# Four output tiles moved from cross-attention into the last self-attention unit, and context keys padded with zeros, in a transformer block on one core

## The chip, the core and the metric

The kernel runs on one core of a Trainium2 chip, in float32 throughout. A time is that of one execution on the device, in microseconds (us); smaller is better. A profile is one execution recorded by the hardware. Its engines are PE (TensorE, matmuls), PEld (its weight loads, beside the matmuls), DVE (VectorE), ACT (ScalarE), POOL (GpSimd) and SP (SyncE, which issues most DMAs).

## What is computed

One transformer block with 16 heads of 64, on x of 2 x 1024 x 256 and a context of 2 x 154 x 192. The inner width of attention is 1024, the feed-forward's is 1024 with a gate.

```python
def _attention(xq, xkv, wq, wk, wv, wo, bo):
    q = (xq @ wq).reshape(B, S, N_HEADS, D_HEAD)
    k = (xkv @ wk).reshape(B, T, N_HEADS, D_HEAD)
    v = (xkv @ wv).reshape(B, T, N_HEADS, D_HEAD)
    attn = softmax(einsum('bihd,bjhd->bhij', q, k) * D_HEAD ** -0.5)
    out = einsum('bhij,bjhd->bihd', attn, v).reshape(B, S, D_ATTN)
    return out @ wo + bo

h = _layernorm(x, ln1_g, ln1_b)
x = _attention(h, h, sa_wq, sa_wk, sa_wv, sa_wo, sa_bo) + x
h = _layernorm(x, ln2_g, ln2_b)
x = _attention(h, cond_emb, ca_wq, ca_wk, ca_wv, ca_wo, ca_bo) + x
h = _layernorm(x, ln3_g, ln3_b)
a, gate = split(h @ ff_w1 + ff_b1)
x = (a * gelu(gate)) @ ff_w2 + ff_b2 + x
```

## The kernel before

All of x stays on chip, as tiles of 128 rows (8 for each of the two batch entries, `xt`), and the three stages run one after the other. Work is cut into units: one batch entry and one pair of heads, 16 units for each attention.

**Self-attention** is a loop over `p` of 128 slots, 8 for each unit, and a slot takes 2 groups of 64 query rows. In `self_first` PE makes the scores (L370) into both buffers of the PSUM pool `ps_s`, DVE takes their maxima over half of the keys (L530), and ACT the exponents with their sums (L381), which frees the scores' banks for the next slot. Two halves of the keys lie on different partitions, so each slot sends maxima and sums to its neighbours by four small DMAs on SP (`exchange`, L391), and a slot later `join` reconciles them: differences on POOL (L399 to L401), the exponent `ee` on ACT (L403), sums on POOL (L405, L407), the reciprocal `rd` on DVE (L477), and POOL weighs the exponents (L481). A slot after that DVE transposes them in 32x32 blocks (L495), and PE multiplies them with the values (`self_values`, L417) in the slots p with p % 4 of 2 or 3. In the slots with p % 4 of 0 or 1 `run_work` gives PE other work: pieces of the next unit from the list `work` (two halves of the queries `q`, the keys, the values), one step of the normalisation that the next stage needs (`side`), and output tiles of attention (`outs`, `out_piece`: four matmuls of 128x256, L348, and a DVE add into x, L355). Banks for these come from the PSUM pool `ps_m`, two buffers. What a piece leaves for ACT is run in the next slot (`stores`), what it leaves for DVE too (`adds`). One closure of `later` is run in each slot; the bias adds on POOL (L255) are among them.

**Cross-attention** is a loop over `c` of 48 slots, 3 for each unit, and a slot takes up to 3 tiles of 128 query rows. Here the scores (L645) are one matmul for each tile and head, 154 wide, followed by maxima (`neg`, L650), exponents (L661), reciprocal (L669), weighing (L672) and transposes into 32x32 blocks (L688). The first five slots also finish the last slots of self-attention (`self_drain`): the weighing of slot 127 in c = 0, its transposes in c = 1, its values in c = 2 and 3. The 154 keys are padded to 5 blocks of 32 in the exponents. For each two pairs of heads the values of the context are made in one piece (`values`, L604 to L619): a memset on POOL of the last block's tile, matmuls for 128 and for 26 rows, and three ACT copies, the last into the memset's tile; then DMAs bring the rows to the other partitions (L621, L626).

The order on every engine is that in which the program emits the instructions: there is no scheduler behind it[...]. The last unit of self-attention is p = 120 to 127. At p = 120 `self_beside` takes the pieces of the first unit of cross-attention:

```python
            work.extend(nxt[:2])
            held.extend(nxt[2:])
```

`held` joins `work` at p = 124. A slot of that unit runs one piece:

```python
                full = hg % 2 == 0 or outs and p < SA - 2 * SH
                run_work(2 if full and p < SA - 2 * SH else 1, 1, sum_tile)
```

So it has q0 in slot 120, q1 in 121, the keys in 124 and the values in 125. Tiles 4 to 7 of the first half of batch entry 1's output come to `outs` at c = 0 (`out_pieces("sa", B - 1, 0, range(NT // 2, NT))`), and the slots of cross-attention take two pieces each, `work` first: one tile in slot 1, two in slot 2, one in slot 4. The heads that they sum were done before the last unit.

The stages that follow are the feed-forward, 64 slots (L809, L815, L818, L832), with the outputs of cross-attention among them.

The names: S = 1024, P = 128, T = 154, KB = 32, NB = 5, NT = 8, SH = 4, SA = 128, NPAIR = 8, CC = 96, VC = 256, NM = 2.

## Time and profile before

| | |
|---|---|
| median of 3 runs | 1179.57 us (1178.59 to 1180.47) |
| the profiled execution | 1178.48 us |
| its span | 1176.6 us |
| PE busy | 1143.3 us (97%) |
| DVE, POOL, ACT busy | 830.9 (71%), 670.7 (57%), 642.9 (55%) us |
| matmuls of the scores (L370) and values (L417) | 256.4 and 236.3 us |
| matmuls of output tiles (py_sa, L348) | 256 records, median 379 ns |
| exponents (L381), weighing (L481) | 345.2 us of ACT, 387.6 us of POOL |
| maxima (L530), transposes (L495) | 301.4 and 302.4 us of DVE |
| granted clock of PE over the span | 0.994 |

The span runs from the first to the last instruction; what lies around it belongs to the execution's own time. A row of the timeline gives the start, the time from its first to its last instruction, the engine, the line, the operation, what is written and read with its size, and the count; brackets hold the idle time of the engine before it and what ended it. A float32 matmul is two records here, so that a tile's four matmuls show as x8. In a row of stretches a busy time is followed by the number of instructions, and 1.00 is the full clock of PE.

### The profile page before, as it was taken

To read this page: it belongs to the slowest core of one execution; us is meant where nothing else is said; L and a number is where in the kernel's file an instruction comes from. 1 tells how busy PE (TensorE), PEld (TensorE's weight loads), DVE (VectorE), ACT (ScalarE), POOL (GpSimd) and SP (SyncE) were. 2 spreads that over 40 slices of the span, in tenths; PEclk is the share of its full clock that TensorE was granted. 3 is DMA by queue.
4 is the path that set the end of the run, shared out by engine and by line. 5 is a ranking of instruction groups with operands and counts; after the bars stand their busy time and mean duration, and the time that the engine had idled before them with its cause. 6 is when DMAs were issued, how large, how long until landed. Compare 5 with 4: busy or idle time off the path is not lost.

```text
span 1176.6 us, 31689 instructions
## 1 busy us (share of the span) xinstructions
PE 1143.3 (97%) x11907; PEld 669.7 (57%) x11907; DVE 830.9 (71%) x1172; ACT 642.9 (55%) x2053; POOL 670.7 (57%) x1563
## 2 busy tenths in 40 slices
PE   7999999999999999999999988999999999999998
PEld 4434445545545545545545433665555567888887
DVE  3888888898888888889999888556655574232222
ACT  3656776666656656656666765456655572041111
POOL 1678777877777777777777777445644453030000
PEclk8999999999999999999999998999999999999999
DMA  2321011011111111111111110176444433000000
GB/s 63 92 61 27 18 27 21 22 33 21 26 25 22 24 25 21 28 22 21 28 23 21 24 21 6 46 173 156 102 107 102 102 80 73 1 19 9 18 10 18
DMA packets 87018, 51.06 MB, mean 43 GB/s; under 512 B 30742, under 2 KB 77650, under 8 KB 86866
## 3 DMA queue, kind: packets, MB, share of 16 engines
q1 hardware_dynamic: 83650, 46.42, 17.4%
q10 hardware_dynamic: 3216, 2.62, 0.7%
q8 instruction: 94, 1.54, 0.6%
q14 instruction: 58, 0.48, 0.1%
HBM read 19.52 MB, written 2.10 MB: 18 GB/s over the span
## 4 chain that ended last, share of the span: by engine, by line
PE 75%; POOL 6%; ACT 6%; DMA 4%; DVE 4%; issue 3%; SPq 2%; ACTq 0%; DVEq 0%; POOLq 0%
PE po L417 14%; PE s L370 13%; PE pa L809 9%; PE py_sa L348 5%; PE py_ca L348 5%; PE pf L832 5%; PE pq_ca L290 4%; ACT p L381 4%; PE poc L721 4%; DMA st<-st 3%; PE pk_sa L290 3%; PE pq_sa L290 3%; PE sc L645 3%; PE pv_sa L305 3%; POOL p L481 3%
## 5 line engine op out<-in xcount | busy, mean ns | idle before, releaser
L381 ACT ACTIVATE p<-s,st 128x512 f32<-128x512 f32 x512 | 345.2, 686 | 219.9 <-DVE st L530 210.4
L481 POOL TENSOR_SCALAR p<-p,rd,ee 128x512 f32<-128x512 f32 x512 | 387.6, 772 | 43.8 <-DVE rd L477 43.2
L530 DVE TENSOR_REDUCE st<-s 128x2 f32<-128x1024 f32 x256 | 301.4, 1219 | 45.9 <-PE s L370 38.1
L495 DVE STREAM_TRANSPOSE pT<-p 128x1024 f32<-128x1024 f32 x256 | 302.4, 1218 | 0.6 <-POOL p L481 0.5
L370 PE MATMUL s<-k_sa,q_sa 64*32 64x512 f32 x4096 | 256.4, 600 | 20.5 <-ACT p L381 19.3
L417 PE MATMUL po<-pT,v_sa 64*64 64x256 f32 x4096 | 236.3, 380 | 1.2 <-DVE pT L495 1.2
L417 PEld LDWEIGHTS po<-pT,v_sa 64*64 64x64 f32 x4096 | 151.0, 133 | 110.5 <-issue 40.4
L672 POOL TENSOR_SCALAR p<-p,rden 128x154 f32<-128x154 f32 x256 | 97.4, 402 | 119.3 <-DVE rden L669 118.1
L370 PEld LDWEIGHTS s<-k_sa,q_sa 64*32 64x32 f32 x4096 | 58.8, 106 | 153.8 <-ACT p L381 67.8
L661 ACT ACTIVATE p<-sc,neg 128x154 f32<-128x154 f32 x256 | 96.0, 394 | 88.6 <-DVE rden L669 84.4
L809 PE MATMUL pa<-hT_ln,wf 128*128 128x256 f32 x512 | 121.0, 379 | 0.0
L818 DVE SCALAR_TENSOR_TENSOR u<-pa,cols,gate 128x256 f32<-128x256 f32 x64 | 31.0, 484 | 124.1 <-ACT gate L815 124.1
L815 ACT ACTIVATE gate<-pa,cols 128x256 f32<-128x256 f32 x64 | 30.3, 474 | 152.1 <-PE pa L809 152.1
L809 PEld LDWEIGHTS pa<-hT_ln,wf 128*128 128x128 f32 x512 | 96.8, 190 | 13.7 <-issue 0.8
L381 ACT ACTIVATION_READ_ACCUMULATOR p<-s,st 128x1 f32 x512 | 103.5, 202 | 0.0
L650 DVE TENSOR_REDUCE neg<-sc 128x6 f32<-128x924 f32 (+1 forms) x48 | 48.6, 1013 | 48.3 <-PE sc L645 48.3
L405 POOL TENSOR_TENSOR zz<-ee,st 128x8 f32<-128x8 f32 x128 | 26.0, 203 | 84.3 <-ACT ee L403 84.3
L305 PEld LDWEIGHTS pv_sa<-sa_wv,hT_ln 128*128 128x128 f32 x512 | 59.3, 192 | 16.3 <-issue 12.9
L832 PE MATMUL pf<-wf,u 128*128 128x256 f32 x256 | 65.0, 379 | 0.2 <-DVE u L818 0.2
L305 PE MATMUL pv_sa<-sa_wv,hT_ln 128*128 128x128 f32 x512 | 62.4, 278 | 0.0
L290 PE MATMUL pq_sa<-hT_ln,sa_wq 128*128 128x512 f32 x128 | 61.2, 621 | 0.6 <-DVE hT_ln L230 0.6
L290 PE MATMUL pk_sa<-hT_ln,sa_wk 128*128 128x512 f32 x128 | 60.7, 610 | 1.2 <-DVE hT_ln L230 1.2
(73 smaller groups left out, 1228.4 us busy)
## 6 DMA issues: line engine op xcount, KB each, us to landing
wf<-pT_ca SPq DMA_DIRECT2D x128, 128.0 KB
st<-st SPq DMA_DIRECT2D x512, 1.0 KB
v_sa<-v_sa SPq DMA_DIRECT2D x64, 128.0 KB
wf<-in_L_xattn_ff_w_dram SPq DMA_DIRECT2D x12, 256.0 KB
sa_wq<-in_L_xattn_sa_wq_dram SPq DMA_DIRECT2D x16, 128.0 KB
sa_wk<-in_L_xattn_sa_wk_dram SPq DMA_DIRECT2D x16, 128.0 KB
sa_wv<-in_L_xattn_sa_wv_dram SPq DMA_DIRECT2D x16, 128.0 KB
ca_wq<-in_L_xattn_ca_wq_dram SPq DMA_DIRECT2D x16, 128.0 KB
```

The costliest lines, as they stand in the source:

```text
L290: nc.tensor.matmul(pq, lhsT=wt[:, c, :], rhs=h[:, c, n * HB:(n + 1) * HB], start=(c == 0), stop=(c == NC - 1),)
L305: nc.tensor.matmul(pv[:, i * P:(i + 1) * P], lhsT=h[:, c, (n * GT + i) * P:(n * GT + i + 1) * P], rhs=wt[:, c, :], start=(c == 0), stop=(c ...
L348: nc.tensor.matmul(py[:, :D], lhsT=o[:, i, t * P:(t + 1) * P], rhs=wo[kind][:, half * HP + i, :], start=(i == 0), stop=(i == HP - 1),)
L370: nc.tensor.matmul(sc[a4 * KB:(a4 + 1) * KB, j, :], lhsT=q[r, c:c + KB], rhs=k[r, h * HB:(h + 1) * HB], start=True, stop=True, tile_positi ...
L381: nc.scalar.activation(pr[:, j, :], sc[:, j, :], AF.Exp, bias=st[:, 0, 0, i, j:j + 1], accum_out=st[:, 0, 1, i, j:j + 1],)
L417: nc.tensor.matmul(po[a2][j * DH:(j + 1) * DH, :QH // 2], lhsT=v[r, t, e, j * DH:(j + 1) * DH], rhs=pT[r, j * NK + n, :], start=(t == 0 an ...
L481: nc.gpsimd.tensor_scalar(pr[:, j, :], pr[:, j, :], rd[:, c:c + 1], ee[:, 0, c:c + 1], op0=ALU.mult, op1=ALU.mult,)
L495: nc.vector.transpose(halves[h][:, :, c:c + KB], groups.pop(0).rearrange("p j (n k) -> p (j n) k", k=KB))
L530: nc.vector.tensor_reduce(st[:, 0, 0, i, :], sc[i], AX.X, ALU.max, negate=True)
L672: nc.gpsimd.tensor_scalar(pr_[:, j, i, :T], pr_[:, j, i, :T], rden[:, j, i:i + 1], 1.0, op0=ALU.mult, op1=ALU.mult,)
L809: nc.tensor.matmul(pa[:, half, :TF * P], lhsT=w1[:, c, half * DF + f * P:half * DF + (f + 1) * P], rhs=h[:, c, t0 * P:(t0 + TF) * P], star ...
L832: nc.tensor.matmul(sums[blk][i][:, :D], lhsT=sums[blk, "u"][:, f, i * P:(i + 1) * P], rhs=w2[:, f, :], start=(f == 0), stop=(f == NF - 1),)
```

## The change

- The padded length TP = 160 replaces T = 154 as the step between the batch entries in the transposed context `ctxT`, and all of `ctxT` is set to zero once at the start, on POOL. The values of the last block come out as zeros beyond row 154, so its matmul, copy and DMAs take 32 rows, and the memset in `values` goes.
- The maxima of cross-attention (`neg`) use the buffers of the tag "zz", 4 wide, in place of their own.
- The four output tiles go into `work` and `held` at p = 120, two and two. The slots of the last unit with p % 4 of 0 or 1 run two pieces each: q0 and q1; tiles 4 and 5; keys and values; tiles 6 and 7. Slot c = 0 runs one piece in place of two.

```diff
+    TP = NB * KB
...
-    ctxT = const.tile([CC, 2, B * T], F32, tag="ctxT", name="ctxT")
+    ctxT = const.tile([CC, 2, B * TP], F32, tag="ctxT", name="ctxT")
+    nc.gpsimd.memset(ctxT, 0.0)
...
-            ctxT[:, :, b * T:(b + 1) * T], pc[:CC, :2 * T].rearrange("p (c k) -> p c k", c=2)
+            ctxT[:, :, b * TP:b * TP + T], pc[:CC, :2 * T].rearrange("p (c k) -> p c k", c=2)
...
-            work.extend(nxt[:2])
-            held.extend(nxt[2:])
+            spare["out"] = mm_tile
+            last = [lambda t=t: out_piece("sa", B - 1, 0, t) for t in range(NT // 2, NT)]
+            work.extend(nxt[:2] + last[:2])
+            held.extend(nxt[2:] + last[2:])
...
-                    rhs=ctxT[:, c, b * T:(b + 1) * T], start=(c == 0), stop=(c == 1),
+                    rhs=ctxT[:, c, b * TP:b * TP + T], start=(c == 0), stop=(c == 1),
...
-            nc.gpsimd.memset(v[:, NM, :], 0.0)
             pv = mm_tile(f"pv_ca{b}_{pr}")
-            m = T - P
-            for n, rows_ in ((0, P), (1, m)):
+            for n, rows_ in ((0, P), (1, KB)):
...
-                        lhsT=ctxT[:, c, b * T + n * P:b * T + n * P + rows_],
+                        lhsT=ctxT[:, c, b * TP + n * P:b * TP + n * P + rows_],
...
-                nc.scalar.copy(v[:m, NM, :], pv[:m, VC:])
+                nc.scalar.copy(v[:KB, NM, :], pv[:KB, VC:])
...
-                    nc.sync.dma_start(out=v[a4 * KB:a4 * KB + m, NM, :], in_=v[:m, NM, :])
+                    nc.sync.dma_start(out=v[a4 * KB:(a4 + 1) * KB, NM, :], in_=v[:KB, NM, :])
...
-        neg = small.tile([P, 2, TG], F32, tag="neg", name=f"neg_{c}")
+        neg = small.tile([P, 2, 4], F32, tag="zz", name=f"neg_{c}")
...
-                full = hg % 2 == 0 or outs and p < SA - 2 * SH
-                run_work(2 if full and p < SA - 2 * SH else 1, 1, sum_tile)
+                full = hg % 2 == 0 or outs or p >= SA - 2 * SH
+                run_work(2 if full else 1, 1, sum_tile)
...
-            if c == 0:
-                out_pieces("sa", B - 1, 0, range(NT // 2, NT))
...
-            run_work(2, 1, n_sum=2 * (SH < c < 2 * NPAIR and c % len(CG) == 0))
+            run_work(2 if c else 1, 1, n_sum=2 * (SH < c < 2 * NPAIR and c % len(CG) == 0))
```

## The prediction

> **What bounds the kernel now.** I read the page first (PE busy 97% of the span, but dips in two slices of the transition from self- to cross-attention), then busy time by stretch over that transition, then the timelines of PE, ACT and POOL inside it, then the granted clock in 1.2 us steps. "Slot p" is one turn of the self-attention loop (p = 120 to 127 is the last unit), "slot c" one of the cross-attention loop. In the stretches the columns are us, then busy us of PE, PEld, DVE, ACT, POOL, the granted clock and DMA.

> ```profile
> 687.61:735.93 48.32, 40.35 (x537) 16.14 (x533) 39.52 (x41) 27.60 (x85) 38.09 (x86) 0.93 0.05 10
> 735.93:764.88 28.95, 27.77 (x244) 18.74 (x241) 14.98 (x24) 13.43 (x60) 14.51 (x37) 1.00 0.15 45
> 764.88:805.00 40.12, 40.12 (x281) 26.32 (x282) 23.78 (x57) 18.85 (x90) 17.40 (x54) 1.00 0.72 178
> ```

> The first row is the last unit: PE is idle for 8.0 of 48.3 us, and POOL and DVE lead. The second is c = 0 to 4: PE idle for only 1.2 us. The third has no idle at all. So PE work is free in the first stretch and sets the end in the other two, where DVE, ACT and POOL are half idle.

> ```profile
> 714.62 1.09 PE L370 MATMUL s<-k_sa,q_sa 64*32 64x512 f32 x16 [2.34 <-ACT p L381]
> ...
> 717.85 2.78 PE L609 MATMUL pv_ca<-ca_wv,ctxT 96*128 96x256 f32 x8
> ...
> 728.58 1.16 PE L370 MATMUL s<-k_sa,q_sa 64*32 64x512 f32 x16 [2.43 <-ACT p L381]
> ...
> 731.80 4.20 PE L417 MATMUL po<-pT,v_sa 64*64 64x256 f32 x64
> ...
> 745.95 3.68 PE L417 MATMUL po<-pT,v_sa 64*64 64x256 f32 x64 [1.18 <-DVE pT L495]
> ...
> 749.56 3.72 PE L348 MATMUL py_sa<-sa_wo,o_sa 128*128 128x256 f32 x16
> ...
> 763.06 1.89 PE L348 MATMUL py_sa<-sa_wo,o_sa 128*128 128x256 f32 x8
> 764.88 0.79 PE L645 MATMUL sc<-k_ca,q_ca 64*128 64x154 f32 x8
> ```

> PE waits for exponents ahead of the scores; two output tiles (x16) stand in slot 2 and one (x8) in slot 4, back to back with the rest.

> ```profile
> 721.85 0.73 ACT L618 COPY v_ca<-pv_ca 64x256 f32<-64x256 f32 x2
> 726.83 0.36 ACT L619 COPY v_ca<-pv_ca 26x256 f32<-26x256 f32 x1 [4.25 <-POOL v_ca L604]
> ```

> ```profile
> 725.81 0.73 POOL L255 TENSOR_TENSOR x<-x,ca_bo 128x256 f32<-128x256 f32 x1
> 726.48 0.32 POOL L604 MEMSET v_ca<- 128x256 f32 x1
> ```

> The memset costs 0.32 us but stands on POOL behind 3.03 us of weighing (L481) and a bias add. ACT's third copy waits 4.25 us for it, and the exponents of slot 126 are queued behind that copy. DVE's maxima start 5.50 us apart from slot 120 to 126 (689.85, 695.35, ... 722.85) and then 8.01 us apart (730.86): the stall costs 2.5 us.

> **The memset and the padding.** Eight memsets leave POOL, 8 x 0.32 = 2.6 us, where POOL has slack; only the first matters, for the 2.5 us above (the others are waited for by 0.5 us in all). The new one, 96x640, stands at the start between the memset of the identity and its select. The identity's memset (128x128) takes 0.20 and the 128x256 one 0.32, so 0.12 per 128 columns: 0.20 + 4 x 0.12 = 0.7 us, an estimate. The warming transposes would then end near 7.3 in place of 6.6, and PE's next work starts at 9.35, released by ACT: hidden by that 2.7 us gap, 0.7 us if it were gone. A shorter gap could also spare some of the half clock that this profile shows from 9.2 to 16.0; between -1.8 (the first query projection takes 3.75 us there, 1.98 later) and +0.7 I take 0, nearest to the gap's row. The values' second matmul, its copy and its three DMAs get 32 rows for 26[...], so no cost. The maxima's tile now rotates with another of four buffers; its earlier users are over two slots old: nothing.

> **The four tiles.** A tile is 1.82 to 1.86 us of PE (3.66 for two, from 749.56 to 753.22) and a DVE add of 0.38 to 0.43. Two go to slot 121 and two to 125, and q1 and the values move up a slot, so slots 120 and 124 hold two pieces. PE's idle time ahead of scores was 1.39, 1.39, 2.59 and 2.60 = 8.0 us in that unit; the tiles need 7.3. Filled, slot 121 runs scores to 695.0, tiles to 698.7, and the next scores, free of their banks at 698.1, come 0.5 us late; DVE needs them only at 700.86. A slot with two pieces is 1.9 + 3.65 = 5.55 us against the loop's 5.50: no loss. Without the idle time the move would only shift 7.3 us.

> The adds stand on DVE ahead of the reciprocal, which POOL's weighing waits for. In slot 122 DVE has 2.36 + 2.36 + 0.8 + 0.2 = 5.7 us of work: +0.2. In slot 126 the same, and that bounds it, for the bias add (0.73) has left POOL's slot 125. So the maxima of slot 126 start at 723.05, those of 127 at 723.05 + 5.7 = 728.75, where it was 730.86: 2.1 us won. PE's last values of the unit end at 731.95, against 735.93: PE is 4.0 us ahead.

> **What is late next.** Slot 2's values (745.95 before) need the transposes of slot 127, and that chain is not shortened by fewer tiles. From 728.75: exponents end 732.7; POOL weighs slot 126 from 733.85 to 736.85; the bias add, moved here, 0.7; differences to 738.45; the ee on ACT 738.7; sums and reciprocal 739.4; weighing 3.03 to 742.65; transpose 1.26, so PE starts at 744.1. Won: 1.85, not 4.0. PE meanwhile does 10.2 us (scores, q0, scores, q1, keys, scores) and is idle some 1.6 us ahead of the keys (whose bank waits for ACT's copy of q0, behind the ee) and 3.3 ahead of the values. On SP the values' DMAs (two of 0.54, three of 0.81 us to issue) now stand ahead of the exchanges of slots 126 and 127; they end near 725.4 and 732.2, the exchanges are ready at 727.1 and 732.7: hidden, by 0.5 us at worst.

> From there PE is the bound, and loses three tiles: before, 745.95 to 764.88 is 18.93 us; 18.93 - 3.66 - 1.82 = 13.45, so slot 5's scores come at 757.55, 7.3 us earlier. In these 13.5 us ACT has some 9, POOL 7 and DVE 8 us of work: still PE. After slot 4 the order on PE is the old one, so 7.3 stay.

> **The clock.** Here the change has something against it. Rows of the granted clock:

> ```profile
> 716.80:718.00 1.20, 1.20 (x17) 0.15 (x1) 0.83 (x2) 0.00 (x0) 0.87 (x2) 0.50 0.06 9
> 718.00:719.20 1.20, 1.20 (x3) 1.02 (x4) 1.20 (x2) 0.59 (x2) 1.20 (x3) 0.50 0.04 2
> ...
> 730.00:731.20 1.20, 1.20 (x16) 0.14 (x16) 0.52 (x2) 0.00 (x0) 0.77 (x3) 0.50 0.08 14
> 731.20:732.40 1.20, 1.20 (x16) 0.42 (x12) 1.20 (x2) 0.28 (x1) 1.20 (x3) 0.50 0.03 1
> ```

> After 2.34 and 2.43 us idle the clock is halved for about 3.4 us each (715.8 to 719.2, 729.5 to 732.9); after 1.18 us at 744.8 it is not. Both halvings fall away with the idle time, but a new one follows slots 1 and 2, now in the PE-bound stage, where half of 3.4 us is 1.7 lost. [...] By the row, 2.4 idle is enough. I take the row, less what of the slow window falls on the wait itself: 1.3. Bounds: 0 and 3.4 (two windows; the start shows 9.2 to 16.0).

> **Sum.** 7.3 - 1.3 = 6.0 us. The profiled execution took 1178.48 (span 1176.6), 1.09 under the median of 1179.57; 1172.5 by its own time, 1173.6 as a median.

> **Rivals.**
> - No half clock after slot 2: 7.3, so 1172.3. For it: the gap is in two pieces with 1.45 us of work between. Against: 4.9 of 6.3 us idle, more than ahead of either halving. Chance 0.20.
> - The tiles were filler: another engine sets c = 2 to 5 once they are gone, and only the 1.85 us to the values remain: 1177.7. For it: ACT's exponents wait for DVE there. Against: those waits end with PE's scores, and PE's records are back to back. Chance 0.13.
> - It doesn't do what it says: the copy waits for more than the memset (say a free V buffer), and the exponents of slot 125 now stall: the 1.85 us are lost and PE's three tiles remain, 5.5 - 1.3 = 4.2: 1175.4. Against: the two copies into the same tile just before it ran at once. Chance 0.05.
> - Slower: the half clock does not let go after slot 2, because PE keeps waiting in slots 3 to 5 as well. Each further 3.4 us cost 1.7; from five windows (8.5 us) it turns 7.3 into a loss, from six (10.2) it gives 1182.5. For it: at the start two windows followed each other. Against: from 749 on PE had no idle time and full clock. Chance 0.03.
> - The main case, 1173.6: chance 0.59. Its own range, 1172 to 1175.5.

> The range 1171.0 to 1177.2 takes the main case, the first and third rivals, the start's 1.8 in part and the second window. About 0.2% (2.4 us) is what a measurement of this kernel can tell from no change: faster (under 1177.2) 0.86, same 0.10, slower 0.04.

> **What would show it.** Right: no L604 row; maxima 5.5 to 5.7 us apart up to slot 127; PE without idle time in the last unit, clock 1.00; slot 2's values wait 3 us or more for L495 and then run near half clock; all after slot 5 earlier by one constant. Wrong: waits of the scores for the exponents stay in slots 121 or 125; the reciprocal waits behind the adds by much over 0.2 us; idle PE between slots 3 and 5; POOL's differences wait for the exchange of slot 127; or the cross stage loses the gain again at its normalisation near 810 us.

## The result and the profile after

The changed kernel takes 1173.43 us in the median of 6 runs (1170.62 to 1174.01), the kernel before 1179.37 us beside it (6 runs, 1177.20 to 1180.48): ratio 0.9948, 95% interval 0.9938 to 0.9959. Predicted were 1173.6. The profiled execution of the changed kernel took 1174.01 us, with a span of 1172.2 and a mean granted clock of 0.994, as before.

The last unit and slots 0 to 4, the first two of the stretches of before, cut at the scores of the same slots, with the same columns. Line numbers lie two to four higher in the changed kernel (scores L372, tiles L350, values L419, transposes L497).

```profile
688.54:732.66 44.12, 43.48 (x568) 21.71 (x565) 39.33 (x45) 26.95 (x83) 36.31 (x81) 1.00 0.06 11
732.66:760.04 27.38, 23.32 (x212) 13.91 (x208) 13.34 (x19) 12.93 (x57) 14.61 (x37) 0.88 0.16 47
```

The last unit is 4.2 us shorter although PE does 3.1 us more in it: its idle time went from 8.0 to 0.6 us, and its clock from 0.93 to 1.00. The next stretch lost three tiles and is only 1.6 us shorter: it has 4.1 us of idle PE, and its clock is 0.88 in place of 1.00. What was wrong with the first stretch has partly moved into the second. PE's timeline shows where:

```profile
715.66 1.09 PE L372 MATMUL s<-k_sa,q_sa 64*32 64x512 f32 x16 [0.40 <-ACT p L383]
...
718.02 3.72 PE L350 MATMUL py_sa<-sa_wo,o_sa 128*128 128x256 f32 x16
...
729.05 3.68 PE L419 MATMUL po<-pT,v_sa 64*64 64x256 f32 x64
...
739.33 0.79 PE L599 MATMUL pk_ca<-ctxT,ca_wk 96*128 96x154 f32 x4 [0.80 <-ACT q_ca L300]
...
744.11 6.07 PE L419 MATMUL po<-pT,v_sa 64*64 64x256 f32 x64 [3.27 <-DVE pT L497]
...
760.04 0.80 PE L647 MATMUL sc<-k_ca,q_ca 64*128 64x154 f32 x8
...
763.24 1.99 PE L350 MATMUL py_sa<-sa_wo,o_sa 128*128 128x256 f32 x8 [0.36 <-ACT k_ca L603]
765.17 1.06 PE L647 MATMUL sc<-k_ca,q_ca 64*128 64x154 f32 x12
```

The two tiles follow slot 125's scores at once, and that wait fell from 2.34 to 0.40 us. The values of slot 127 (729.05) run in 3.68 us where they took 4.20. Slot 2's values wait 3.27 us for the transpose of slot 127 and then take 6.07 us, where the same matmuls (x64) took 3.68 before.

ACT's copies of the context's values run one after the other. The memset is gone, and with it the wait of 4.25 us; the third copy takes 0.36 us for 32 rows as it did for 26, and the values' matmuls have a median of 379 ns in both kernels:

```profile
717.56 0.74 ACT L620 COPY v_ca<-pv_ca 64x256 f32<-64x256 f32 x2
718.32 0.36 ACT L621 COPY v_ca<-pv_ca 32x256 f32<-32x256 f32 x1
```

**Where the time went.** Both traces are set at the scores of slot 120, PE's first row of the last unit (687.61 before, 688.54 after), and read at the first cross scores of slot 5 (764.88 and 760.04): 77.27 us before, 71.50 after, 5.77 won. This is 2.77 won up to slot 2's values (58.34 to 55.57), 5.48 of PE for the three tiles that left slots 2 and 4, less 2.39 lost in slot 2's values and 0.09 in small things. In slot 5 itself 0.44 is lost: the tile that stayed there (763.24) now waits 0.36 us for ACT's copy of the keys, which frees its bank. That leaves 5.33. From slot 5's first row of 1.06 us (769.57 before, 765.17 after) to the end the two run 4.4 us apart (spans 1176.6 and 1172.2). The 0.93 us between 5.33 and 4.40 had been lost ahead of slot 120; the run with the context's memset moved, below, bears on why.

### The profile page after: what moved, and what is told of

Same layout as the page of the kernel before. It is cut to its first block, busy times and chain, and to the rows that moved or that the text cites. A ratio compares the mean times of both kernels' runs of the same rounds, so it can differ in the third digit from the quotient of the medians.

```text
span 1172.2 us, 31665 instructions
## 1 busy us (share of the span) xinstructions
PE 1141.8 (97%) x11907; PEld 670.2 (57%) x11907; DVE 830.0 (71%) x1172; ACT 643.4 (55%) x2053; POOL 665.9 (57%) x1556
## 4 chain that ended last, share of the span: by engine, by line
PE 76%; ACT 6%; POOL 5%; DVE 4%; DMA 3%; issue 3%; SPq 2%; ACTq 0%; DVEq 0%; POOLq 0%
PE po L419 14%; PE s L372 14%; PE pa L811 9%; PE py_ca L350 5%; PE pf L834 5%; PE py_sa L350 4%; PE pq_ca L292 4%; ACT p L383 4%; PE poc L723 4%; PE pq_sa L292 4%; PE pk_sa L292 4%; PE pv_sa L307 3%; PE sc L647 3%; DMA st<-st 3%; POOL p L483 3%
## 5 line engine op out<-in xcount | busy, mean ns | idle before, releaser
L497 DVE STREAM_TRANSPOSE pT<-p 128x1024 f32<-128x1024 f32 x256 | 302.4, 1219 | 1.7 <-POOL p L483 1.7
L372 PE MATMUL s<-k_sa,q_sa 64*32 64x512 f32 x4096 | 253.9, 596 | 13.2 <-ACT p L383 12.2
L419 PE MATMUL po<-pT,v_sa 64*64 64x256 f32 x4096 | 238.2, 382 | 3.3 <-DVE pT L497 3.3
L419 PEld LDWEIGHTS po<-pT,v_sa 64*64 64x64 f32 x4096 | 151.8, 134 | 112.8 <-issue 43.0
L372 PEld LDWEIGHTS s<-k_sa,q_sa 64*32 64x32 f32 x4096 | 59.3, 105 | 144.5 <-ACT p L383 59.1
```

What stands on the lines that cost most here:

```text
L372: nc.tensor.matmul(sc[a4 * KB:(a4 + 1) * KB, j, :], lhsT=q[r, c:c + KB], rhs=k[r, h * HB:(h + 1) * HB], start=True, stop=True, tile_positi ...
L419: nc.tensor.matmul(po[a2][j * DH:(j + 1) * DH, :QH // 2], lhsT=v[r, t, e, j * DH:(j + 1) * DH], rhs=pT[r, j * NK + n, :], start=(t == 0 an ...
L497: nc.vector.transpose(halves[h][:, :, c:c + KB], groups.pop(0).rearrange("p j (n k) -> p (j n) k", k=KB))
```

## The experiments

Ratios are to the kernel before, timed beside each run. "The ledger" is the same reading of a profile: scores of slot 120 to the first cross scores of slot 5, less the 77.27 us of before. Seven matmuls of 128x256 that write a bank nobody reads serve as filler in some runs; they take 3.2 to 3.3 us at full clock.

**The padding alone** (all of the change but the move of the tiles, which stay in slots 1, 2 and 4):

```diff
+    nc.gpsimd.memset(ctxT, 0.0)
...
-            nc.gpsimd.memset(v[:, NM, :], 0.0)
```

> The padding alone: no memset of the values in the loop, one of the padded context at the start; the four tiles stay in slots c = 1 to 4. My theory: the 2.5 us stall of slot 126 goes, the maxima stay 5.50 us apart to slot 127, slot 2's values start about 2.5 us earlier from slot 120 on, and PE, which has the tiles between, waits for them 1 to 2 us; everything after is as before. So about 2.5 us under before (ratio near 0.998), between before and the changed kernel. Rival 'the memset does nothing for the end, all comes from the tiles': 0. Rival 'the stall is all of it': 6 us.

Measured: 1176.67 us, 21 runs, against 1179.40; ratio 0.9977, interval 0.9971 to 0.9984, so 2.7 us. Ledger: 3.05. The maxima of the last unit lie 5.49 to 5.59 us apart without the 8.01. PE:

```profile
717.67 3.29 PE L372 MATMUL s<-k_sa,q_sa 64*32 64x512 f32 x32 [2.44 <-ACT p L383]
...
745.77 3.68 PE L419 MATMUL po<-pT,v_sa 64*64 64x256 f32 x64 [1.55 <-DVE pT L497]
```

The clock was still halved behind 2.44 us of idle PE: scores that take 1.95 elsewhere took 3.29. That cost nothing, since PE is not what sets the pace there: the maxima stay 5.5 us apart. In slot 2 PE waited 1.55 us, and the values took 3.68 us, as at full clock.

**The tiles alone** (the context buffer and the memset as before):

```diff
-            work.extend(nxt[:2])
-            held.extend(nxt[2:])
...
+            work.extend(nxt[:2] + last[:2])
+            held.extend(nxt[2:] + last[2:])
```

> The move of the four tiles alone, with the memset kept in the values' piece, which now stands in slot 124. My theory: ACT's copy in slot 125 waits for the memset some 4 us behind the weighing on POOL and slot 125 to 126 takes about 8 us in place of 5.5; slot 2's values start about as before, and three tiles are gone behind them (5.5 us), less the half clock: about 3.5 us under before (2.5 to 4.5), 2.5 above the changed kernel. Rival 'PE's work in the last unit hides the stall': as the changed kernel, 6 us under before. Rival 'the tiles were filler': no gain.

Measured: 1177.87 us, 21 runs; ratio 0.9988, interval 0.9982 to 0.9995: 1.4 us, less than half of what I expected. With the loss in slot 5 its ledger says 2.99 - 0.44 = 2.55. First ACT, then PE:

```profile
722.81 0.36 ACT L621 COPY v_ca<-pv_ca 26x256 f32<-26x256 f32 x1 [4.06 <-POOL v_ca L606]
```

```profile
723.23 1.99 PE L348 MATMUL py_sa<-sa_wo,o_sa 128*128 128x256 f32 x8 [2.78 <-ACT v_ca L621]
...
747.12 6.29 PE L417 MATMUL po<-pT,v_sa 64*64 64x256 f32 x64 [3.28 <-DVE pT L495]
```

The stall on the memset is still there (maxima 8.01 us apart, one slot earlier), and now PE stands 2.78 us between two tiles, because the second needs the bank that ACT's stalled copy reads. Slot 2's values take 6.29 us. The two parts of the change need each other: 2.7 and 1.4 us make 4.1 of the change's 5.9 (by the ratios, 0.0035 of 0.0052; the intervals leave this difference clear of noise only narrowly, and the wait of 2.78 us is what shows it).

**Filler ahead of slot 2's values**, in the changed kernel:

```diff
+            if c == 2:
+                fill = sum_tile("fill")
+                for _ in range(7):
+                    nc.tensor.matmul(
+                        fill[:, :2 * P], lhsT=ident, rhs=hT["ca", 0][:, 0, :2 * P], start=True, stop=True)
```

> The changed kernel with seven matmuls more that nobody reads (128x256, 0.43 us each, 3.0 us), into a bank of the sums, between slot 2's scores and its values, where PE waits 3.3 us. My theory: the long run of slot 2's values (6.07 us for 3.68) is the half clock that the idle time brings. With PE busy the clock stays at 1.00, the values take 3.7, and the whole is up to 2.4 us shorter than the changed kernel although it has more work: ratio to before about 0.993. If the wait in slot 1 (0.8 to 1.6 us) is enough to halve the clock, the gain is under 1 us. Rival 'the long run has another cause' (DMA traffic, banks, weights): the values still take 6 us and the whole is the same or up to 0.5 us longer.

Measured: 1171.82 us, 5 runs; ratio 0.9935, interval 0.9923 to 0.9948. It wins nothing for the chain (the values start 15.14 us after slot 127's maxima, 14.98 without filler), but they take 3.68 us, and the clock is 1.00 in every stretch from 737.0 to 751.4:

```profile
742.28 3.29 PE L934 MATMUL fill<-hT_ln,ident 128*128 128x256 f32 x14
745.63 3.68 PE L419 MATMUL po<-pT,v_sa 64*64 64x256 f32 x64
```

Ledger: 7.67, against 5.77. Slot 2's values are 2.39 us shorter, and 0.48 us of that is lost ahead of them: slot 127's maxima come 0.32 later from slot 120 on and the chain takes 0.16 more. So the long run of slot 2's values was the half clock, not the matmuls or their operands. By the times the filler wins 1.5 us over the change (0.0013), and the intervals overlap a little (0.9923 to 0.9948, 0.9938 to 0.9959); the run with the tiles alone and this filler, below, shows the effect by times.

**Tiles 6 and 7 in slot 0** of cross-attention in place of slot 125:

```diff
-            held.extend(nxt[2:] + last[2:])
+            held.extend(nxt[2:])
+            gap.extend(last[2:])
...
+            if c == 0:
+                run(work.pop(0))
+                spare["out"] = sum_tile
+                for piece in gap:
+                    run(piece)
```

> The changed kernel, but tiles 6 and 7 are run in slot c = 0 behind q0, in the two banks of the sums, in place of slot 125. My theory: they fit into PE's wait ahead of slot 2's values (4 us idle), which are set by the chain of slot 127 and stay where they are; the clock stays full, so about 2.4 us under the changed kernel, ratio to before about 0.993. Slot 125 then has 1 to 2 us of PE idle time, which should cost nothing. Rival 'the chain passes through PE': the second scores come 3.7 us later, the maxima and exponents behind them delay the transposes of slot 127, and the whole is 1 to 3 us above the changed kernel.

Measured: 1173.05 us, 5 runs; ratio 0.9944, interval 0.9928 to 0.9960, so no better than the change, where I expected 0.993.

```profile
721.26 3.67 PE L372 MATMUL s<-k_sa,q_sa 64*32 64x512 f32 x32 [3.05 <-ACT p L383]
724.86 4.83 PE L419 MATMUL po<-pT,v_sa 64*64 64x256 f32 x64
...
746.09 3.69 PE L419 MATMUL po<-pT,v_sa 64*64 64x256 f32 x64 [0.40 <-DVE pT L497]
```

The wait in slot 2 is gone as expected, and its values run at full clock. But slot 125 without tiles leaves PE idle for 3.05 us, and the clock is 0.50 there from 720.4 to 727.2. Scores of 3.67 and values of 4.83 us do not fit the loop's 5.5: the maxima of slot 127 come 6.90 us after those of 126, where the change has 5.27. My expectation that idle PE in the last unit is free was wrong.

**The same with filler in slot 125** (seven matmuls after the pieces of that slot):

```diff
+                if p == SA - SH + 1:
+                    fill = sum_tile("fill")
...
```

> The kernel with tiles 6 and 7 in slot c = 0, and seven matmuls that nobody reads (3.0 us) in slot 125, where PE had 3.05 us of idle time in that kernel and the clock was halved behind it. My theory: the half clock made slot 126 take 6.9 us in place of 5.3 and took back 1.6 us; with PE busy there, slot 126 to 127 takes 5.3 to 5.5 us and the whole is about 1.5 us under that kernel, ratio to before 0.993. Rival 'the slot is long because tiles 6 and 7 are no longer there for another reason': as before the fill, 0.9944.

Measured: 1170.55 us, 5 runs against 1179.29; ratio 0.9927, interval 0.9914 to 0.9939. Maxima of slots 126 and 127 are 5.04 us apart, 6.90 without the filler, and slot 126's scores and values take 2.33 and 3.69 us for 3.67 and 4.83. The interval overlaps at the edge with that of the run without filler (0.9928 to 0.9960), so the profiles carry this reading, and the times agree with it.

**No bias add on POOL in slot 127**, with six filler matmuls in slot 2:

```diff
-            if later:
+            if later and p < SA - 1:
```

> The kernel with the gap filled by matmuls that nobody reads (six of them now), and the bias add that the change brought into slot 127 put off to slot c = 0, behind the weighing of slot 127. My theory: the add stands on the chain that slot 2's values wait for, so they start 0.7 us earlier after slot 127's maxima (14.3 us for 15.0), and the whole is 0.7 us under the kernel with seven matmuls: ratio to before about 0.993. Rival 'the differences of slot 127 wait for their DMAs anyway': at most 0.2 us.

Measured: 1170.93 us, 5 runs; ratio 0.9929, interval 0.9917 to 0.9942. The values start 14.28 us after slot 127's maxima (728.88 to 743.16), against 15.14 with seven matmuls and 14.98 in the change: the bias add (0.73 us at 737.10 in the change) did stand in the chain from slot 127 to slot 2. By the times alone this run and the one with seven matmuls can't be told apart.

**The context's memset behind the select of the identity**, so that the warming transposes do not wait for it:

```diff
-    nc.gpsimd.memset(ctxT, 0.0)
...
+        nc.gpsimd.memset(ctxT, 0.0)
```

> The changed kernel with the memset of the padded context behind the first normalisation on POOL, so that the identity and the warming transposes are 0.6 us earlier, as before the change. My theory: the gap of 2.7 us behind the transposes hid that: no difference to the changed kernel (within 0.5 us, ratio to before 0.9948). Rival 'the later start of the transposes costs time': up to 1 us under the changed kernel.

Measured: 1173.49 us, 5 runs; ratio 0.9946, interval 0.9933 to 0.9958, no different from the change, though the intervals would hide an effect of 1 us or a little more. What differs at the start between profiles is where the first half clock falls: from 9.3 to 16.1 us before, from 11.7 to 18.5 in the change. In the change the keys' projection (`pk_sa`) falls into it too. This happens without the memset too: the profile of the tiles alone, which has no such memset, shows the keys' projection at 3.08 us, like the change's 3.17, and the filler run, which has it, at 1.89. The first scores begin between 22.7 and 24.4 us in the seven profiles with the 0.63 us memset ahead, and between 22.6 and 24.0 in the five without. So the memset's place is not seen to cost anything, and the 0.93 us of the change's profile look like chance. Over all profiles slot 120's scores begin between 687.5 and 690.5.

This profile is a second look at the change's order, and it shows what the wait of slot 2 costs in another execution:

```profile
743.11 5.29 PE L418 MATMUL po<-pT,v_sa 64*64 64x256 f32 x64 [3.26 <-DVE pT L496]
```

After the same wait the values take 1.61 us over 3.68 in place of 2.39, and the ledger is 6.46.

**The tiles spread out**: q0 alone in slot 120, a tile with q1 in 121, a tile with the keys in 124, the context's values alone in 125, two tiles in slot 0:

```diff
+            work.extend(nxt[:2] + last[:1])
+            held.extend(nxt[2:3] + last[1:2] + nxt[3:])
+            gap.extend(last[2:])
...
+                run_work(2 if full and p not in (SA - 2 * SH, SA - SH + 1) else 1, 1, sum_tile)
```

with slot 0 as in the run with tiles 6 and 7 there.

> No matmuls without use: the four tiles are laid so that PE is never idle for over about 1.4 us. Slot 120 has q0, slot 121 q1 and tile 4, slot 124 the keys and tile 5, slot 125 the values, slot c = 0 q0 of the next unit and tiles 6 and 7 in the banks of the sums. By this order slot 127 has no bias add either. My theory: the clock stays at 1.00 from slot 120 to slot 5, the maxima are 5.5 us apart, and slot 2's values follow those of slot 127 by 14.3 to 15.2 us: about as the changed kernel with the gap filled, 7.5 us under before, ratio 0.9935. Rival 'idle time of 1.1 to 1.4 us in slots 120, 124 and 125 is enough to halve the clock': 1 to 3 us above that.

Measured: 1170.77 us, 5 runs against 1179.29; ratio 0.9922, interval 0.9909 to 0.9936, under that of the change (0.9938 to 0.9959). It needs no matmul that nobody reads.

```profile
721.65 1.09 PE L372 MATMUL s<-k_sa,q_sa 64*32 64x512 f32 x16 [1.00 <-ACT p L383]
...
744.10 3.68 PE L419 MATMUL po<-pT,v_sa 64*64 64x256 f32 x64 [0.40 <-DVE pT L497]
```

No wait of PE from slot 120 to slot 5 is longer than 1.0 us, and the stretches show the clock at 1.00 in both stages:

```profile
689.50:733.12 43.62, 40.45 (x553) 18.55 (x549) 38.90 (x43) 26.92 (x83) 36.97 (x81) 1.00 0.04 8
733.12:757.65 24.53, 24.13 (x229) 15.60 (x225) 14.15 (x22) 13.19 (x59) 14.15 (x38) 1.00 0.20 59
```

The last unit still has 3.2 us of idle PE, in waits of at most 1.0 us with the clock at 1.00, and the PE-bound stage 0.4. Ledger: 9.12, 3.35 more than the change: 2.38 from slot 2's values on, where the half clock was, 0.73 in the chain, which no longer has the bias add in it (slot 127's maxima to slot 2's values: 14.25 us for 14.98), and 0.24 before it.

**The tiles alone, filled**, to settle what the second run left open: first the filler ahead of slot 2's values, then the same seven matmuls between the two tiles of slot 125 as well.

```diff
+            if c == 2:
+                fill = sum_tile("fill")
...
-                run_work(2 if full else 1, 1, sum_tile)
+                if p == SA - SH + 1:
+                    run_work(1, 1, sum_tile)
+                    fill = sum_tile("fill")
...
+                    run_work(1, 0, sum_tile)
+                else:
+                    run_work(2 if full else 1, 1, sum_tile)
```

> This is the run with the four tiles alone (the context buffer as before, with its memset of the values) plus seven matmuls of 128x256 that nobody reads, put before slot 2's last values, where that run's PE stood still 3.3 us and then took 6.29 us for values that take 3.68 at full clock. Theory (the tiles alone gained only 1.4 us because the half clock behind this wait takes back 2 to 2.4 us): the values take 3.7 us again and the time is 3.5 to 4 us under the kernel before, a ratio near 0.997. Rival (what is missing is elsewhere, and the wait of slot 2's chain is all that counts): 1.4 us under the kernel before, as without them, ratio 0.999.

> The run before this one, plus seven more such matmuls between the two tiles of slot 125, where PE waited 2.78 us for ACT's copy of the context's values. Theory (in most executions of the tiles alone that wait falls so that the clock is halved behind it as well, and that is the rest of the gain that was missing): about 5 us under the kernel before, ratio near 0.9957, which is what the profiled execution of the tiles alone gives when the half clock behind slot 2 is given back (2.99 - 0.44 + 2.4). Rival (the rest isn't the clock): the same as the run before this one.

Measured against 1179.78 (23 runs): 1175.66, 10 runs, ratio 0.9966, interval 0.9955 to 0.9977; and 1175.16, 13 runs, ratio 0.9964, interval 0.9955 to 0.9973. The first filler gives back 0.9988 - 0.9966 = 0.0022 of the time, 2.6 us, and its interval lies clear of the one without it. So the half clock of slot 2 shows here by times as well. The second filler adds 0.2 to 0.5 us, which the runs can't tell from nothing. In the profiles it does give something: the first of the two halved the clock behind the same wait in slot 125, with maxima 9.07 us apart, and the second did not, with 8.00 (scores of 1.95 us at 725.68, where the first took 2.93 at 725.46). So that loss exists in some executions; how often it occurs, and whether it is the rest of the second run's shortfall, stays open.

## Why the prediction was right, step by step

- **The stall of slot 126** was put at 2.5 us. Right: the padding alone gives 2.7 (1.9 to 3.4 by the interval).
- **The four tiles fill idle time** of the last unit. Right: 8.0 us of idle time became 0.6, at full clock.
- **The adds on DVE** were to cost 0.2 us in slots 122 and 126 each, with slot 127's maxima 5.7 us after those of 126. They came 5.27 after, and with the adds of slot 122 the next step was 5.47:

```profile
723.86 2.35 DVE L532 TENSOR_REDUCE st<-s 128x2 f32<-128x1024 f32 x2
726.13 2.36 DVE L497 STREAM_TRANSPOSE pT<-p 128x1024 f32<-128x1024 f32 x2
728.42 0.72 DVE L357 TENSOR_TENSOR x<-py_sa,x 128x256 f32<-128x256 f32 x2
729.06 0.16 DVE L479 RECIPROCAL rd<-den 128x4 f32<-128x4 f32 x1
729.13 2.32 DVE L532 TENSOR_REDUCE st<-s 128x2 f32<-128x1024 f32 x2
```

  A step from one start to the next is shorter than the row: 2.27, 2.29, 0.64 and 0.07 us, which is 5.27, where I had added up durations. So 2.66 us were won at slot 127's maxima rather than 2.1 (730.86 and 729.13, each from its slot 120).
- **The chain from there to slot 2's values** was to take 15.35 us (728.75 to 744.1) and took 14.98, the bias add in it. Won: 2.77, not 1.85. PE was to wait 1.6 us ahead of the keys and 3.3 ahead of the values; the waits were 0.80 and 3.27. (The 10.2 us of PE work given there don't fit the pieces listed: by the prediction's own starts these are 12.15 - 4.9, some 7.3 us. Nothing else rests on the figure.)
- **Three tiles leave the PE-bound stage**, 5.48 us. Right: outside slot 2's values the stretch from there to slot 5 is 5.39 us shorter. This speaks against the rival that they were filler: PE did the work of slots 2 to 4 without new idle time.
- **The half clock** was put at 1.3 us, within bounds of 0 and 3.4. In this profile it cost 2.39, over 6.8 us:

```profile
741.20:742.40 1.20, 0.00 (x0) 0.00 (x0) 1.18 (x1) 1.20 (x8) 1.20 (x2) 0.90 0.26 76
742.40:743.60 1.20, 0.00 (x0) 0.00 (x0) 0.95 (x2) 1.20 (x6) 1.20 (x4) 0.50 0.00 0
...
747.20:748.40 1.20, 1.20 (x16) 0.74 (x12) 0.00 (x0) 0.00 (x0) 0.10 (x2) 0.50 0.00 0
748.40:749.60 1.20, 1.20 (x24) 0.87 (x20) 0.00 (x0) 0.00 (x0) 0.00 (x0) 0.75 0.00 0
```

  It set in during the wait at 742.2 and lasted until 749.0, 6.8 us; the first 1.9 fell on idle time, and half of the 4.9 that remained is 2.4. The rival without a half clock is excluded in this profile. The cost differs from execution to execution: in the profile with the context's memset moved the same order lost 1.61, and by the times the filler gave back 1.5 here and 2.6 with the tiles alone. So 1.3 was too small against all of these. For the size of the wait the reading from the rows of before held: the clock was halved behind 2.34 us of idle time there, behind 2.44 with the padding alone, and behind 3.27 here.
- **The wait in slot 5**, 0.44 us, was not foreseen: after slot 4 the order on PE is the old one, but with slot 4's tile gone the copy of the keys is no longer done when slot 5's tile wants its bank.
- **The start** was put at 0. Nothing in the times speaks against it. The profiled execution lost 0.93 us ahead of slot 120, which is part of why it shows 4.5 us and the medians 5.9.

So the mechanism held, and the sum of 6.0 against 5.33 in the profile's ledger hides sizes that were off in opposite directions: 0.9 us more won in the chain, 1.1 more lost to the clock, and 0.44 lost beyond that. That the median came within 0.2 us of the forecast is luck: the errors cancel in part, and the clock's share differs from execution to execution.

## What to carry to other kernels

Work that is moved out of a PE-bound stage wins its length only if PE stays fed there: a wait on another engine's chain costs itself, and here the clock was halved for 3.4 or 6.8 us around waits of 2.34 to 3.28 us, though not at each of them. Spread the moved pieces, instead of filling one stage and emptying the next: of the same four tiles, the spread order, with no wait over 1.0 us and a clock of 1.00, wins 9.2 us and the order of the change 6.1 (ratios 0.9922 and 0.9948 of 1179), and 0.7 of the difference is the bias add that it also takes out of slot 127. A cheap fill can cost as much as the work that its engine has queued ahead of it: 0.32 us of memset cost the loop 2.5.

## What the runs showed of the hardware

The length of the wait alone does not settle it. Behind the same wait in slot 125 (2.78 and 2.77 us) the clock stayed at 1.00 in the run with the tiles alone (first) and was halved in the one with the filler in slot 2 (second):

```profile
723.80:725.00 1.20, 1.20 (x7) 0.91 (x5) 0.00 (x0) 1.20 (x5) 0.00 (x0) 1.00 0.10 20
```

```profile
723.80:725.00 1.20, 1.20 (x6) 0.86 (x4) 0.00 (x0) 1.20 (x5) 0.00 (x0) 0.63 0.06 14
725.00:726.20 1.20, 1.20 (x10) 0.23 (x16) 0.00 (x0) 0.61 (x3) 0.41 (x2) 0.50 0.00 0
```

An early unit shows such a difference too. In the filler run of the changed kernel the second of two scores took 1.60 us behind waits of 1.64 and 0.24 us:

```profile
79.20 1.09 PE L372 MATMUL s<-k_sa,q_sa 64*32 64x512 f32 x16 [1.64 <-ACT p L383]
80.53 1.60 PE L372 MATMUL s<-k_sa,q_sa 64*32 64x512 f32 x16 [0.24 <-ACT p L383]
```

The kernel before has the same two waits there (1.64 and 0.25); its second scores took 1.09 us, and its clock is 1.00 from 72 to 84. What decides between the two outcomes was not shown: no run varied the idle time by itself.
